# The six left-over channels of a depthwise convolution: four images in one matmul group instead of one image per group

## The chip, the cores and the metric

The kernel runs on one core of a Trainium2 chip. The metric is device time in microseconds (us) of one whole execution, all four layers of the network included. The time before is 3689.4 us, the median of three runs of 3689.62, 3683.67 and 3689.40 us.

## What is computed

The reference is four layers, each adding a function of a group-normalised input to its own input. The change lies in the first part of the first layer, which is cut here to what it computes:

```
x: 8 images, 384 channels, 32 x 32 pixels, float32
g = group_norm(x)                        # 32 groups of 12 channels, per image
for p in q, k, v:
    y = depthwise 3x3 convolution of g with dw_p, zero padding 1
    y = batch_norm(y)                    # mean and variance over all 8 images
    p = pw_p @ gelu(y)                   # 384 x 384 projection
attention over the 1024 pixels, 8 heads; projection; batch_norm; + x
then three further layers (experts, quantised convolution, attention with sampled keys)
```

The batch norm needs the mean and variance of each convolved channel over all eight images. So nothing behind the convolution can begin before the convolution of the last image is done. This first stage, all convolutions and their statistics, takes the first 384 us of the profile, and the projections and the attention of the first layer follow it.

## The kernel before

**How the convolution is laid out.** Channel 3p+c lies on partition p of chunk c, so an image is 128 partitions x 3 chunks x 1024 pixels. TensorE does the convolution for q, k and v at once. A group is 42 channels (`GC`): a tile `st` of 126 partitions holds these 42 channels three times, shifted by one row up, not at all, and one row down (`stack`, L311). A weight matrix of 126 x 126 then sums over the three rows and gives 42 x 3 output rows for q, k and v. Three matmuls, one for each column shift (`TAPS`, L334), add up in a PSUM bank, and this is done for the two halves of the image (`h`): six matmuls in the program for each group. In float32 each of them is two passes in the profile, so a group shows as twelve.

**Regular groups and the left-over group.** Nine groups of 42 channels (`NGC`) cover partitions 0 to 125. Partitions 126 and 127 hold six channels (`GR`) which fit in none, and each image has a tenth, left-over group for these, which comes fourth in image 0 and first in the others. Its tile `sr` has 3 x 6 = 18 rows in partitions 0 to 17 and the same 18 rows again in partitions 32 to 49. The first copy serves the first half of the image and the second copy the other half. In the program the matmuls of the two halves alternate (L382), but a scheduler gives out the final order on each engine. The program that is built keeps the alternation for images 2, 4, 6 and 7, and puts the three matmuls of the first half ahead of the three of the second for images 0, 1, 3 and 5.

**What happens around a group.** Six DMAs of SyncE's queue (SP) fill the left-over tile, three fill a regular one (L318, L327). ScalarE (ACT) copies each half from PSUM to the tile `y` (L397), VectorE (DVE) takes the batch-norm statistics of the half into `cst` (L398), and three DMAs on ACT's queue store q, k and v to the DRAM tensors `raw` (L406). On the last image, the stores of groups 5, 6 and 7 go by GpSimd's queue (POOL). For images 0, 2, 4 and 6 (`ON_V`), VectorE computes groups 6, 7 and 8 itself (`convolve`, L275), in 27 taps per image and three closing steps, two of these 30 behind each group. So TensorE has 60 regular and 8 left-over groups.

**Normalisation.** `norm` (L248) makes the group norm of an image in three steps: VectorE takes statistics of the loaded image `xa` into `mv_a`; TensorE sums them over groups in a tiny matmul `gna` (L114), VectorE makes `dm_a`, TensorE sums again in `gnb` (L125); VectorE and GpSimd (L95) make the scale, and ScalarE writes the scaled image to `pad` (L144), from which `stack` reads. These steps of later images are put between the groups of earlier ones. The list `work` holds the order of groups; `begins` (L341) sets behind which group each image's `norm` starts, about 11 groups ahead of its first use. A group's stack is issued 9 groups ahead (`AHEAD`). `y` has 9 buffers, `st` 10, `pad` 2, and the matmul results have 4 PSUM banks.

**End of the stage.** Behind each group of the last image, `bn_moments` (L152) reduces the statistics of that group over all images. `bn_params` (L156) then makes the scales of all ten groups, and two matmuls (`pmove`, L434, L438) bring them into the layout of the next stage.

**DMA semaphores.** In the built program the DMAs of SP and ACT use eight semaphores in turn. A DMA waits until the earlier one with its semaphore has landed. GpSimd's DMAs have eight of their own.

Of the kernel before, what the change touches and what calls it, by code (L numbers as in the profile page):

```python
# [7 lines left out]
F32 = mybir.dt.float32  # L8
# [4 lines left out]
B, C, H, W = 8, 384, 32, 32  # L13
# [4 lines left out]
NT8 = N // P  # L18


GC, NGC, GR = 42, 9, 6

# [30 lines left out]
def tile_kernel(ctx: ExitStack, tc: tile.TileContext, i: dict, out: bass.AP):  # L53
    nc = tc.nc
# [97 lines left out]
    def bn_moments(st, j, tiles):  # L152

        nc.vector.bn_aggr(tiles[0][:, j, :], st[:, j, :, :].rearrange("p a b -> p (a b)"))
# [49 lines left out]
    raw = [dram.tile([B, P, KC, N], F32, name=f"raw{v}") for v in range(3)]  # L204
    ss0 = const.tile([P, 3, 2, KC], F32, name="ss0")
    xmv = const.tile([P, B, KC, 2], F32, name="xmv")
    bn0 = bn_tiles(3 * GC, NGC + 1, "qkv")
    ON_V = (0, 2, 4, 6)
# [8 lines left out]
    with ExitStack() as pa:  # L217
        wa = pa.enter_context(tc.tile_pool(name="a_w", bufs=1))
        sa = pa.enter_context(tc.tile_pool(name="a_s", bufs=10))
# [7 lines left out]
        pads = []  # L227
# [4 lines left out]
        cst = wa.tile([3 * GC, NGC + 1, 2 * B, 6], F32, name="cst")  # L232
# [9 lines left out]
        cw = wa.tile([3 * GC, NGC, 3, 3 * GC], F32, name="cw_sb")  # L242
        nc.sync.dma_start(out=cw[:, :3], in_=i["cw"][:, :3])
        cwv = load_a("cwv")
        cwr = load_a("cwr")
# [65 lines left out]
        def stack(b, g):  # L311

            padf = pads[b % 2].rearrange("p c h w -> p c (h w)")
            if g < NGC:
                st = sa.tile([3 * GC, H, W], F32, tag="st", name=f"st{b}_{g}")
                c, t = divmod(g, 3)
                for dy in range(3):
                    stacked[0] = nc.sync.dma_start(  # L318
                        out=st[dy : 3 * GC : 3].rearrange("p h w -> p (h w)"),
                        in_=padf[t : 3 * GC : 3, c, dy * W : (dy + H) * W],  # L320
                    )
            else:
                st = sa.tile([32 + 3 * GR, H, W], F32, tag="sr", name=f"st{b}_{g}", bufs=2)
                for h in range(2):
                    for dy in range(3):
                        r = 32 * h + dy * GR
                        nc.sync.dma_start(  # L327
                            out=st[r : r + GR].rearrange("p h w -> p (h w)"),
                            in_=padf[3 * GC :, :, dy * W : (dy + H) * W],
                        )  # L330
            return st


        TAPS = [(1, 0, W, 0), (0, 0, W - 1, 1), (2, 1, W, 0)]  # L334
        AHEAD = 9
        groups = [(NGC, *range(NGC - 3 if b in ON_V else NGC)) for b in range(B)]

        groups[0] = (*groups[0][1:4], NGC, *groups[0][4:])
        work = [(b, g) for b in range(B) for g in groups[b]]

        begins = {max(2, work.index((b, NGC)) - AHEAD - 2): b for b in range(1, B)}  # L341
        sts, taps, todo, later, normed = {}, [], {}, list(work), {0}
        stacked = [None]

# [19 lines left out]
        for n, (b, g) in enumerate(work):  # L364
            if n in begins:
                b2 = begins[n]
                for k, f in enumerate(norm(b2)):
                    todo[n + k] = f, (b2 if k == 2 else 0)
                if b2 + 1 < B and b2 + 1 not in xts:
                    load_x(b2 + 1)  # L370
            if n in todo:
                f, b2 = todo.pop(n)
                f()
                normed.add(b2)
            stacks(n + AHEAD + 1)
            st = sts.pop((b, g))
            nch = GC if g < NGC else GR
            y = ya.tile([3 * nch, N], F32, tag="y", name=f"y{b}_{g}")
            pk = [bank(f"pk{b}_{g}_{h}") for h in range(2)]
            steps = [(h, k) for h in range(2) for k in range(3)]  # L380
            if g == NGC:
                steps = [(h, k) for k in range(3) for h in range(2)]  # L382
            for h, k in steps:
                dx, c0, c1, o0 = TAPS[k]
                rows = slice(h * (H // 2), (h + 1) * (H // 2))
                if g < NGC:
                    lhs, rhs = cw[:, g, dx, :], st[:, rows, c0:c1]
                else:
                    r = slice(32 * h, 32 * h + 3 * GR)
                    lhs, rhs = cwr[r, dx, :], st[r, rows, c0:c1]  # L390
                nc.tensor.matmul(  # L391
                    pk[h].rearrange("p (h w) -> p h w", w=W)[: 3 * nch, :, o0 : o0 + c1 - c0],
                    lhsT=lhs, rhs=rhs, start=(k == 0), stop=(k == 2),
                )
                if k == 2:
                    hs = slice(h * HALF, (h + 1) * HALF)
                    nc.scalar.copy(y[:, hs], pk[h][: 3 * nch, :])  # L397
                    nc.vector.bn_stats(cst[: 3 * nch, g, 2 * b + h, :], y[:, hs])  # L398
            for v in range(3):
                if g < NGC:  # L400
                    to, of = raw[v][b, g % 3 : 3 * GC : 3, g // 3, :], y[v : 3 * GC : 3, :]
                else:
                    to, of = raw[v][b, 3 * GC :, :, :], y[v * GR : (v + 1) * GR, :]

                queue = nc.gpsimd if b == B - 1 and g in (5, 6, 7) else nc.scalar
                queue.dma_start(out=to, in_=of)  # L406
            for _ in range(2):
                if taps:
                    taps.pop(0)()
            if b == B - 1:  # L410
                if g == 5:
                    load_b(0)
                bn_moments(cst, g, bn0)
        assert not taps and not todo and not xts


# [85 lines left out]
    with ExitStack() as pb:  # L502
# [179 lines left out]
        for v in range(2):  # L682
# [6 lines left out]
        steps = [  # L689
            (b, pr, h, kc)  # L690
            for b in range(B) for pr in ORDER[b + 1 == B] for h in range(2)
            for kc in range(0, NT8, NS)
        ]
# [66 lines left out]
        for k in range(2):  # L760
            qs = slice(k * HALF // 2, (k + 1) * HALF // 2)
            for m in range(KC):
                for c in range(KC):
                    nc.tensor.matmul(
                        pos[m][:, qs], lhsT=wo0[:, c, m * P : (m + 1) * P],
                        rhs=atts[B - 1][:, c, HALF:][:, qs], start=(c == 0), stop=(c == KC - 1),
# [18 lines left out]
    _, sco, sho = sc_o  # L785
# [51 lines left out]
    with tc.If(redo > 0):  # L837
        with ExitStack() as pb:
            wb = pb.enter_context(tc.tile_pool(name="e_w", bufs=1))
            work = [fetched[divmod(k, 2)] for k in range(5)]  # L840
# [11 lines left out]
            with tc.For_i(0, B) as bi:  # L852
                act = []
                for v in range(3):
                    g = work[v]
                    nc.sync.dma_start(
                        out=g, in_=raw[v][bass.ds(bi, 1)].rearrange("o p c n -> p (o c) n")
# [17 lines left out]
                for v in range(2):  # L875
                    ts = qp.tile([P, NPAIR0, N], F32, tag=f"qk{v}", name=f"qk{v}_e")
                    for pr in range(KC):
                        for h in range(2):
                            pq = bank(f"pq{v}_e{pr}_{h}")
                            for c in range(KC):  # L880
                                nc.tensor.matmul(
                                    pq, lhsT=w_in[v][:, c, pr * P : (pr + 1) * P],
                                    rhs=act[v][:, c, h * HALF : (h + 1) * HALF],
# [9 lines left out]
                for pr in range(NPAIR0):  # L893
                    qt, kt = qks[0][:, pr, :], qks[1][:, pr, :]
                    for h in range(2):
                        pav = bank(f"pav_e{pr}_{h}")
                        for j, r in enumerate(HR):
                            hd = 2 * pr + j
                            pt = qp.tile([P, NT8, HALF], F32, tag="pt", name=f"pt_e{pr}_{h}_{j}")
                            for qc in range(4):  # L900
# [11 lines left out]
                                p = pp.tile([P, N], F32, tag="p", name=f"p{nm}")  # L912
# [14 lines left out]
                            for kc in range(NT8):  # L927
# [5 lines left out]
                                    rhs=pt[:, kc, :],  # L933
# [3 lines left out]
                        hs = slice(h * HALF, (h + 1) * HALF)  # L937
# [913 lines left out]
def _layouts(a):  # L1851
    import numpy as np

    f = np.float32
    L = {}
# [18 lines left out]
    rest, ch = dw[:, NGC * GC :], np.arange(GR)  # L1874
    w = np.zeros((3, GR, 3, 3, GR), f)
    w[:, ch, :, :, ch] = rest.transpose(1, 2, 3, 0)
    w = w.reshape(3 * GR, 3, 3 * GR)
    dwv = np.stack([a[f"L0_conv_dw_{n}"].reshape(P, KC, 9)[:, KC - 1] for n in "qkv"])
    L["cwv"] = dwv.transpose(1, 0, 2)
    L["cwr"] = np.concatenate([w, np.zeros((32 - 3 * GR, 3, 3 * GR), f), w])  # L1880
    gb = np.zeros((3 * GC, 2, NGC + 1), f)
    for k, t in enumerate("gb"):
        v = np.stack([a[f"L0_conv_{t}_{n}"][order] for n in "qkv"])
# [83 lines left out]
```

## Time and profile before

| | |
|---|---|
| runs of the kernel before | 3689.62, 3683.67, 3689.40 us; median 3689.4 |
| the profiled execution | 3684.65 us, span 3682.8 us |
| TensorE (PE) busy | 3569.8 us, 97% of the span |
| VectorE, ScalarE, GpSimd busy | 48%, 35%, 5% of the span |
| mean granted TensorE clock | 0.982 |
| the first stage, to its last convolution matmul | 383 us; VectorE's last statistics start at 384.4 us |
| regular group's matmul passes `pk<-st,cw_sb` | 720 |
| left-over group's matmul passes `pk<-st,cwr_sb` | 96 |

Times are microseconds from the start of the span, means and medians in ns where marked. PE is a matmul pass and PEld its weight load. Matmuls overlap and their ends are modelled, so how far apart the weight loads start tells more than how long a matmul lasts. In the timeline, each row is start, duration, engine, line, operation, output<-input, count, and in brackets how long the engine was idle ahead of it and what ended that. `<-issue` names no wait that the profile could see. SPq and ACTq are the DMA queues of SyncE and ScalarE.

### The profile page before, as it was taken

What the parts mean: (1) busy time and instruction counts of PE and PEld (TensorE: products, weight loads), DVE (VectorE), ACT (ScalarE), POOL (GpSimd) and SP (SyncE); (2) the same over time, 40 slices, a digit from 0 to 9 for tenths busy, and PEclk for the clock granted to TensorE, in tenths of its full rate; (3) what the DMA queues carried; (4) which work ended last, traced back from release to release, by engine and by line L of the source; (5) the groups of instructions that cost most, each with busy time, mean ns of one, the idle gap of its engine ahead of it and who ended that gap; (6) DMA issues with size and microseconds to landing.
All of it is one profiled execution on the core that took longest, in us unless ns stands there. A gap on an engine that the chain in (4) does not pass through costs nothing.

```text
span 3682.8 us, 39040 instructions
## 1 busy us (share of the span) xinstructions
PE 3569.8 (97%) x15605; PEld 1525.8 (41%) x15605; DVE 1765.5 (48%) x2835; ACT 1273.8 (35%) x1524; POOL 196.1 (5%) x162
## 2 busy tenths in 40 slices
PE   7999999999999999999899999999999999999887
PEld 3444333333333333334434444445344444444434
DVE  6776223232323232323437637475663657547563
ACT  2222354545454444544322222323323232322222
POOL 0000100000000000000000010100102010010112
PEclk9999999999999999999999999999999999999898
DMA  6676311111212120212350010010101001010000
GB/s 205 229 253 228 146 55 34 66 42 58 64 37 64 39 77 27 76 27 74 112 218 23 33 52 20 33 54 33 37 20 48 37 33 43 28 52 20 0 35 18
DMA packets 88179, 253.33 MB, mean 69 GB/s; under 512 B 19114, under 2 KB 19706, under 8 KB 87602
## 3 DMA queue, kind: packets, MB, share of 16 engines
q1 hardware_dynamic: 75000, 211.35, 17.3%
q10 hardware_dynamic: 12408, 37.78, 3.0%
q8 instruction: 127, 2.08, 0.2%
q0 software_dynamic: 576, 1.55, 0.1%
q14 instruction: 68, 0.56, 0.0%
HBM read 133.39 MB, written 75.59 MB: 57 GB/s over the span
## 4 chain that ended last, share of the span: by engine, by line
PE 40%; DVE 9%; ACT 1%; DMA 0%; issue 0%; POOL 0%; DVEq 0%; POOLq 0%; ACTq 0%; SPq 0%
PE y L1327 12%; PE ph L1306 8%; DVE y L1402 6%; PE pq L1447 3%; PE pf L1737 3%; PE pw L1410 3%; PE pav L1637 2%; PE s L1621 2%; DVE hd L1292 1%; PE pss L1650 1%; PE pk L1595 1%; PE pv L1604 1%; PE xsb L1581 1%; PE px L1470 1%; DVE off L1517 1%; PE plog L1056 0%
## 5 line engine op out<-in xcount | busy, mean ns | idle before, releaser
L661 ACT ACTIVATE p<-s 128x1024 f32<-128x1024 f32 x512 | 496.4, 1021 | 508.7 <-PE s L654 508.4
L1327 PE MATMUL y<-hd,w_sb 128*128 128x512 f32 x1080 | 490.5, 600 | 3.5 <-DVE hd L1292 3.5
L669 PE MATMUL pav<-p,vt 64*64 64x512 f32 x4096 | 489.1, 590 | 0.0
L1306 PE MATMUL ph<-h,w_sb 128*128 128x512 f32 x1104 | 485.2, 594 | 1.0 <-DMA w_sb<-in_w_dram 0.9
L654 PE MATMUL s<-qk,qk 48*64 48x512 f32 x3072 | 371.9, 597 | 3.3 <-ACT p L661 3.3
L391 PE MATMUL pk<-st,cw_sb 126*126 126x512 f32 x720 | 320.5, 607 | 11.2 <-DMA st<-pad 10.4
L1306 PEld LDWEIGHTS ph<-h,w_sb 128*128 128x128 f32 x1104 | 207.5, 190 | 260.2 <-issue 255.9
L1327 PEld LDWEIGHTS y<-hd,w_sb 128*128 128x128 f32 x1080 | 198.5, 191 | 245.1 <-issue 233.5
L669 PEld LDWEIGHTS pav<-p,vt 64*64 64x64 f32 x4096 | 165.4, 133 | 276.3 <-issue 268.1
L630 DVE COPY ta<-pav 128x512 f32<-128x512 f32 (+1 forms) x65 | 44.2, 682 | 411.1 <-PE pav L669 411.1
L1402 DVE SCALAR_TENSOR_TENSOR y<-h,tap,y 128x961 f32<-128x961 f32 (+1 forms) x192 | 233.5, 1239 | 0.6
L1316 ACT ACTIVATE hd<-ph,b_sb 128x512 f32<-128x512 f32 x180 | 122.8, 682 | 316.0 <-PE ph L1306 316.0
L391 PEld LDWEIGHTS pk<-st,cw_sb 126*126 126x126 f32 x720 | 139.6, 196 | 183.9 <-issue 180.3
L1517 DVE SCALAR_TENSOR_TENSOR off<-q,dw_sb,off 128x225 f32<-128x225 f32 (+3 forms) x432 | 211.9, 546 | 1.6
L654 PEld LDWEIGHTS s<-qk,qk 48*64 48x64 f32 x3072 | 112.7, 133 | 227.0 <-issue 184.1
L78 DVE COPY qk<-pq 128x512 f32<-128x512 f32 x48 | 33.2, 692 | 292.6 <-PE pq L571 292.6
L397 ACT COPY y<-pk 126x512 f32<-126x512 f32 (+1 forms) x136 | 76.1, 584 | 252.5 <-DMA raw<-y 104.0
L1628 ACT ACTIVATE p<-s 128x1024 f32<-128x1024 f32 x96 | 93.3, 1022 | 191.0 <-PE s L1621 190.9
L1292 DVE TENSOR_TENSOR hd<-hd,cb 128x512 f32<-128x512 f32 x180 | 122.2, 684 | 47.9 <-ACT hd L1316 47.7
L1410 PE MATMUL pw<-y,upw 128*128 128x512 f32 x288 | 129.4, 603 | 9.3 <-DVE y L1402 9.3
L1737 PE MATMUL pf<-att,wp_sb 128*128 128x512 f32 x288 | 130.3, 607 | 4.3 <-DVE att L1664 3.8
L571 PE MATMUL pq<-g,wq_sb 128*128 128x512 f32 x288 | 131.0, 605 | 2.3 <-DMA wq_sb<-in_wq_dram 2.3
(292 smaller groups left out, 3830.1 us busy)
## 6 DMA issues: line engine op xcount, KB each, us to landing
g<-raw SPq DMA_DIRECT2D x72, 512.0 KB
st<-pad SPq DMA_DIRECT2D x180, 168.0 KB
raw<-y ACTq DMA_DIRECT2D x171, 168.0 KB
xa<-in_x_dram SPq DMA_DIRECT2D x24, 512.0 KB
xh<-in_x_dram SPq DMA_DIRECT2D x48, 256.0 KB
f<-in_x_dram SPq DMA_DIRECT2D x24, 512.0 KB
f<-o SPq DMA_DIRECT2D x24, 512.0 KB
o<-ot SPq DMA_DIRECT2D x42, 256.0 KB
```

The costliest lines, as they stand in the source:

```text
L391: nc.tensor.matmul(pk[h].rearrange("p (h w) -> p h w", w=W)[: 3 * nch, :, o0 : o0 + c1 - c0], lhsT=lhs, rhs=rhs, start=(k == 0), stop=(k = ...
L571: nc.tensor.matmul(pq, lhsT=w_in[v][:, c, pr * P : (pr + 1) * P], rhs=acts[b][v][:, c, h * HALF : (h + 1) * HALF], start=(c == 0), stop=(c ...
L654: nc.tensor.matmul(s[64 * k : 64 * k + 64, j * HALF : (j + 1) * HALF], lhsT=kt[r, k0 : k0 + 64], rhs=qt[r, h * HALF : (h + 1) * HALF], sta ...
L661: nc.scalar.activation(p, s, AF.Exp, scale=scale)
L669: nc.tensor.matmul(pav[k][64 * j : 64 * j + 64, :], lhsT=vts[b % 2][r, kc, 2 * hd : 2 * hd + 2, :].rearrange("p a b -> p (a b)"), rhs=p[r, ...
L1292: nc.vector.tensor_tensor(hd, hd, state["cb"], ALU.mult)
L1306: nc.tensor.matmul(ph, lhsT=w1[:, e, c, dc * P : (dc + 1) * P], rhs=state["h1"][c], start=(c == 0), stop=(c == KC - 1),)
L1327: nc.tensor.matmul(y, lhsT=w2[:, e, dc, m * P : (m + 1) * P], rhs=state[h, k], start=(k == 0), stop=(k == NE * KC - 1),)
L1402: nc.vector.scalar_tensor_tensor(d, f, tap2[:, c, t : t + 1], d, ALU.mult, ALU.add)
L1410: nc.tensor.matmul(pw[h], lhsT=upw2[:, c, m * P : (m + 1) * P], rhs=y[c][:, hs], start=(c == 0), stop=(c == KC - 1),)
L1517: nc.vector.scalar_tensor_tensor(d, f, dw3[:, t : t + 1], d, ALU.mult, ALU.add)
L1737: nc.tensor.matmul(pf[:, hs], lhsT=wp3[:, pr, m * P : (m + 1) * P], rhs=att[:, pr, hs], start=(pr == 0), stop=(pr == NPAIR3 - 1),)
```

## The change

The left-over channels of four images (`BR`) go into one tile of 4 x 18 = 72 partitions and are convolved as one group, with a block-diagonal weight matrix of 72 x 72. This group comes first in images 3 and 7; the other images have none. `left_over` issues three DMAs per image instead of six, behind the stack of group 1 (for images 3 and 7, ahead of group 0). The statistics of the group go into a tile `stl` first. GpSimd's queue then issues, for each of the four images, three stores to `raw` and one DMA that brings 18 rows of statistics to their place in `cst`: 16 DMAs for each such group. The reduction of the left-over statistics moves behind group 5 of the last image. The list `work` has 62 groups instead of 68, and the places where `norm` begins are computed anew.

```diff
-GC, NGC, GR = 42, 9, 6
+GC, NGC, GR, BR = 42, 9, 6, 4
...
+                if g == 1 and (b + 1) % BR:
+                    left_over(b)
             else:
-                st = sa.tile([32 + 3 * GR, H, W], F32, tag="sr", name=f"st{b}_{g}", bufs=2)
-                for h in range(2):
-                    for dy in range(3):
-                        r = 32 * h + dy * GR
-                        nc.sync.dma_start(
-                            out=st[r : r + GR].rearrange("p h w -> p (h w)"),
-                            in_=padf[3 * GC :, :, dy * W : (dy + H) * W],
-                        )
+                left_over(b)
+                st = lefts.pop(b // BR)
             return st
+        lefts = {}
+        def left_over(b):
+            k, j = divmod(b, BR)
+            if j == 0:
+                lefts[k] = sa.tile([3 * GR * BR, H, W], F32, tag="sr", name=f"sr{k}", bufs=2)
+            padf = pads[b % 2].rearrange("p c h w -> p c (h w)")
+            for dy in range(3):
+                r = (3 * j + dy) * GR
+                nc.sync.dma_start(
+                    out=lefts[k][r : r + GR].rearrange("p h w -> p (h w)"),
+                    in_=padf[3 * GC :, :, dy * W : (dy + H) * W],
+                )
...
-        groups = [(NGC, *range(NGC - 3 if b in ON_V else NGC)) for b in range(B)]
-        groups[0] = (*groups[0][1:4], NGC, *groups[0][4:])
+        groups = [
+            (*range(NGC, NGC + (b % BR == BR - 1)), *range(NGC - 3 if b in ON_V else NGC))
+            for b in range(B)
+        ]
         work = [(b, g) for b in range(B) for g in groups[b]]
-        begins = {max(2, work.index((b, NGC)) - AHEAD - 2): b for b in range(1, B)}
+        begins, n = {}, -1
+        for b in range(1, B):
+            n = max(n + 3, work.index((b, groups[b][0])) - AHEAD - 2)
+            begins[n] = b
...
-            nch = GC if g < NGC else GR
+            nch = GC if g < NGC else GR * BR
...
             if g == NGC:
-                steps = [(h, k) for k in range(3) for h in range(2)]
+                stl = wa.tile([3 * GR * BR, 2, 6], F32, tag="stl", name=f"stl{b}")
             for h, k in steps:
...
-                    r = slice(32 * h, 32 * h + 3 * GR)
-                    lhs, rhs = cwr[r, dx, :], st[r, rows, c0:c1]
+                lhs = cw[:, g, dx, :] if g < NGC else cwr[:, dx, :]
+                rhs = st[:, rows, c0:c1]
...
-                    nc.vector.bn_stats(cst[: 3 * nch, g, 2 * b + h, :], y[:, hs])
+                    st1 = cst[:, g, 2 * b + h, :] if g < NGC else stl[:, h, :]
+                    nc.vector.bn_stats(st1, y[:, hs])
+            for k in range(3 * BR if g == NGC else 0):
+                (j, v), r = divmod(k, 3), k * GR
+                b1 = b + 1 - BR + j
+                nc.gpsimd.dma_start(out=raw[v][b1, 3 * GC :, :, :], in_=y[r : r + GR, :])
+                if v == 0:
+                    nc.gpsimd.dma_start(
+                        out=cst[: 3 * GR, NGC, 2 * b1 : 2 * b1 + 2, :],
+                        in_=stl[r : r + 3 * GR, :, :],
+                    )
...
-                bn_moments(cst, g, bn0)
+                for k in () if g == NGC else (g, NGC) if g == 5 else (g,):
+                    bn_moments(cst, k, bn0)
```

In the built program of the changed kernel all six matmuls of the new group stand in the order first half, second half. On GpSimd its 16 DMAs stand behind the normalisation step of image 4, and those of the second group behind that of image 7. The order of the instructions behind this stage differs on no engine except for the place of one set of three small statistics DMAs on SP.

More of the change, by code (lines that the diff above doesn't have):

```diff
@@ L385, in tile_kernel @@
                 rows = slice(h * (H // 2), (h + 1) * (H // 2))
-                if g < NGC:
-                    lhs, rhs = cw[:, g, dx, :], st[:, rows, c0:c1]
-                else:
-                    r = slice(32 * h, 32 * h + 3 * GR)
-                    lhs, rhs = cwr[r, dx, :], st[r, rows, c0:c1]
+                lhs = cw[:, g, dx, :] if g < NGC else cwr[:, dx, :]
+                rhs = st[:, rows, c0:c1]
                 nc.tensor.matmul(
@@ L397, in tile_kernel @@
                     nc.scalar.copy(y[:, hs], pk[h][: 3 * nch, :])
[L398 to L403, printed above, removed]
+                    st1 = cst[:, g, 2 * b + h, :] if g < NGC else stl[:, h, :]
[9 more added lines that the diff above has]
+                    )
+            for v in range(3 if g < NGC else 0):
+                to, of = raw[v][b, g % 3 : 3 * GC : 3, g // 3, :], y[v : 3 * GC : 3, :]
                 queue = nc.gpsimd if b == B - 1 and g in (5, 6, 7) else nc.scalar
@@ L1876, in _layouts @@
     w[:, ch, :, :, ch] = rest.transpose(1, 2, 3, 0)
-    w = w.reshape(3 * GR, 3, 3 * GR)
+    w, wr = w.reshape(3 * GR, 3, 3 * GR), np.zeros((BR, 3 * GR, 3, BR, 3 * GR), f)
+    for j in range(BR):
+        wr[j, :, :, j] = w
     dwv = np.stack([a[f"L0_conv_dw_{n}"].reshape(P, KC, 9)[:, KC - 1] for n in "qkv"])
     L["cwv"] = dwv.transpose(1, 0, 2)
-    L["cwr"] = np.concatenate([w, np.zeros((32 - 3 * GR, 3, 3 * GR), f), w])
+    L["cwr"] = wr.reshape(3 * GR * BR, 3, 3 * GR * BR)
     gb = np.zeros((3 * GC, 2, NGC + 1), f)
```

## The prediction

> **What bounds the kernel now.** First the page: TensorE is busy for 97% of the span, so any time must come from its own queue. Then the stretches of the first stage (columns: stretch and length, busy time of PE, PEld, DVE, ACT, POOL with instruction counts, clock, DMA share, GB/s):
>
> ```profile
> 18.00:104.00 86.00, 79.49 (x176) 32.54 (x176) 63.65 (x99) 22.97 (x34) 1.11 (x2) 0.92 0.69 225
> 104.00:285.00 181.00, 174.06 (x425) 74.94 (x426) 135.02 (x202) 51.32 (x80) 3.89 (x4) 0.95 0.71 236
> 285.00:384.00 99.00, 98.72 (x244) 42.47 (x244) 60.39 (x85) 25.75 (x43) 6.12 (x10) 0.98 0.74 256
> ```
>
> PE is nearly full in all three, but its clock falls below 1.00. Then the weight loads, since their spacing is the true pace of PE. First the left-over group of image 6, whose halves alternate, and then that of image 3, whose halves stand one behind the other:
>
> ```profile
> 302.35 0.12 PEld L391 LDWEIGHTS pk<-st,cwr_sb 18*18 18x18 f32 x4 [0.73 <-issue]
> 302.80 0.10 PEld L391 LDWEIGHTS pk<-st,cwr_sb 18*18 18x18 f32 x2 [0.33 <-issue]
> ...
> 304.98 0.29 PEld L391 LDWEIGHTS pk<-st,cw_sb 126*126 126x126 f32 x2 [0.82 <-ACT y L397]
> ```
>
> ```profile
> 156.58 0.11 PEld L391 LDWEIGHTS pk<-st,cwr_sb 18*18 18x18 f32 x2
> 157.02 0.09 PEld L391 LDWEIGHTS pk<-st,cwr_sb 18*18 18x18 f32 x1 [0.34 <-issue]
> ...
> 160.96 0.30 PEld L125 LDWEIGHTS gnb_a<-dm_a,g_sb 128*128 128x128 f32 x2 [0.82 <-DVE cst L398]
> 161.18 0.30 PEld L391 LDWEIGHTS pk<-st,cw_sb 126*126 126x126 f32 x2
> 161.72 0.19 PEld L391 LDWEIGHTS pk<-st,cw_sb 126*126 126x126 f32 x1 [0.24 <-issue]
> 162.15 0.32 PEld L391 LDWEIGHTS pk<-st,cw_sb 126*126 126x126 f32 x1 [0.24 <-issue]
> 162.96 0.34 PEld L391 LDWEIGHTS pk<-st,cw_sb 126*126 126x126 f32 x1 [0.49 <-issue]
> 163.79 0.34 PEld L391 LDWEIGHTS pk<-st,cw_sb 126*126 126x126 f32 x1 [0.49 <-issue]
> ```
>
> The alternating group takes 304.98-302.35 = 2.63 us, two passes going at once. The serial one takes 161.18-156.58 = 4.60, and then four regular passes stand 0.82 apart instead of 0.42: half the clock. This follows every serial left-over group and no alternating one. Last, two weight loads that wait for a normalisation, and VectorE's statistics behind the second wait:
>
> ```profile
> 104.36 0.50 PEld L114 LDWEIGHTS gna_a<-mv_a,g_sb 128*128 128x128 f32 x2 [3.20 <-issue]
> 284.78 0.50 PEld L114 LDWEIGHTS gna_a<-mv_a,g_sb 128*128 128x128 f32 x2 [6.63 <-issue]
> ```
>
> ```profile
> 273.37 1.29 DVE L103 BATCH_NORM_STATS2 st_a<-xa 128x6 f32<-128x512 f32 x2 [8.20 <-DMA xa<-in_x_dram]
> ```
>
> PE works in order: if VectorE's mean is late, all convolutions stand still behind `gna`. At 284.78 the image itself was late.
>
> [...] The trace has nine such DMAs, 0.53 us of queue each (4.8 us), landing in 6.5 us.
>
> **Part 1: left-over matmuls.** Removed, from the first left-over weight load to the next regular one: images 0, 1, 3, 5 (serial) 6.82, 5.60, 4.60, 4.29; images 2, 4, 6, 7 four times 2.63. Sum 31.8. It holds four `gnb` of 0.42 us that stay: 30.1. It also holds `gnb`'s waits of 1.6 us for VectorE in images 0 and 1; a regular group of 5.04 us takes the place between `gna` and `gnb` and hides these. The slow passes behind the serial ones go too: 2.1 us each behind images 0 and 1, 1.65 each behind 3 and 5 = 7.5. Added: two groups of twelve passes at the regular 0.42 us = 10.1[...]. The clock under 72 rows is not in the trace: if they count as idle, each group is followed by 1.7 us more (3.4 us at half), 3.4 in all; if as work, nothing. I take nothing, because attention's 48- and 64-row passes keep the full clock (1.00 from 400 to 500 us). Net 27.5, if nothing else becomes late.
>
> **Part 2: what is late next.** *Image 1's stack.* Without its left-over group, image 0 ends early: group 2 begins at 33.2 as now, then four groups of 5.04 and two tiny matmuls of 0.42, so image 1 begins at 54.2 instead of 69.5. Its norm: `gnb` at 44, 1.5 us to the scale, ScalarE's three 1.24 us passes to 49.5. SP's stack DMAs go out at 1.34 us each there (9 in 12.06), land some 2.3 us later, and the three new left-over DMAs stand between the stacks of groups 1 and 2. Groups 0 and 1 come in time, group 2 some 2 us late. Cost 2.
>
> *Image 3's `gna`.* In the new order it stands behind group 4 of image 1, and VectorE does behind that group's second half: its statistics (with ScalarE's copy, 1.3), three taps of 1.24, six input statistics of 0.6, and the aggregates (0.5). That is 9.1 us in which PE has nothing ahead of it; now the wait is 3.2. Cost 5.9. Its half-clock stretch is there in both.
>
> *Image 7's `gna`.* Now 6.6 us late. In the new order VectorE does the six statistics nearly in one piece (some 5 us from the arrival at 273.4, against 11.2 now), but `gna` comes one group, 5 us, earlier. SP saves about as much as PE does (24 of its DMAs), so the image is about as late: wait 5.2. Gain 1.4. For images 4, 5 and 6 the mean's last input is a group at least two groups ahead of `gna`: nothing.
>
> **Part 3: ScalarE, VectorE, SP.** ScalarE loses 12 copies of 0.57 and 24 stores of about 0.8 us, VectorE 12 statistics of 0.67, SP 24 DMAs of 0.67. All lie beside PE, whose waits for these (0.1 to 0.9 us each) are inside the intervals above. Nothing more is counted.
>
> **Part 4: GpSimd's queue, a new wait.** Each group issues 16 DMAs. Behind the first eight, each waits for the landing of one eight ahead. Estimate from the nine DMAs in the trace: two times eight at 0.53, and two landings of 6.5 = 21 us as the upper end[...]. Behind them on GpSimd stand image 5's scale (for group 3) and the stores of groups 5 to 7 (for image 7). Image 5's `gnb` comes 30 us later: hidden. For image 7, VectorE's aggregate of the left-over channels waits for `cst`; it stands in the middle of group 4, 4.5 x 5.04 = 22.7 us behind the left-over group. Were it later, the work behind it on VectorE (one tap, two and nine statistics, five aggregates: 11 us) still has PE's 22.7 us to fit in: 11 more to spare. Cost 0; beyond some 34 us it would lie on the path one for one. Below nothing it can't go: nobody waited for these stores before. The order behind the stage is the old one, so the 3299 us from 384 on are counted unchanged.
>
> **Sum.** 27.5 - 2 - 5.9 + 1.4 = 21. On the profiled execution 3684.65 - 21 = 3663.7. That execution lies 4.7 us below the median of the runs, 3689.4, which itself is close to two of three; the mean of all four is 3686.8, and I forecast 3686.8 - 21 = 3666 us.
>
> **Rivals.**
> *A: the waits don't come.* If SP, relieved of 24 DMAs, brings images and stacks early and the scheduler's order does no harm, both losses (7.9) and image 7's rest (5.2 and its 1.65 of half clock) go: 21 + 14.8 = 36 gained, 3651. For it: SP's DMA issue runs almost without a break from 13 to 357 us. Against it: the 9.1 us are VectorE's work, not a transfer.
> *B: normalisation bounds the stage, and the gain turns into waits.* If `gna` of images 4 to 6, too, waited 4 us with 1.7 us of half clock each (17), and the 72-row groups halved the clock (3.4), the gain is 21 - 20.4 = 0.6: 3686. For it: two of seven waits stand there now. Against it: in the new order these three means are ready early.
> *C: slower, by GpSimd's queue.* If its 16 DMAs go one by one, each landing (6.5 us) ahead of the next, the left-over statistics of image 7 come after 16 x 6.5 = 104 us, 70 beyond the cover of 34: 3666 + 70 = 3736. It decides from 34/16 = 2.1 us per DMA and makes the kernel slower from (34+21)/16 = 3.4. Against it: three such DMAs were issued within 1.76 us at 371.15.
> *D: the change doesn't do what it says*, and the scheduler splits or repeats the groups: excluded, the built program has 62 groups.
>
> **Chances.** Faster, slower and same are parted at 0.2% (7.4 us), about what a measurement of this kernel can tell from no change. Forecast (13 to 29 us gained) 0.60; A (29 to 40) 0.18; between forecast and B (7.4 to 13) 0.10; B 0.07; C or the like 0.05. Faster 0.88, same 0.07, slower 0.05. The range from 3648 (A, taken from the lowest run, 3683.7) to 3680 (7 us gained) leaves out C, B and the far end of A.
>
> **What would show it.** `pk<-sr,cwr_sb` must have 24 passes instead of 96, 0.42 us apart. The last convolution pass must end about 21 us earlier than 383.5, and the first projection as much before 392.5. The regular passes behind the new groups should stand 0.42 apart (0.83 if 72 rows count as idle). Image 3's `gna` must show about 9 us of idle time, near 91 us. GpSimd's 16 DMAs should end within 21 us of their start, and no aggregate may wait for them. The prediction is wrong if `gna` of images 4 to 6 waits, if a stack is late beyond image 1, or if the gain isn't in the first 400 us.

## The result and the profile after

The changed kernel takes 3666.7 us, the median of five runs (3666.0 to 3667.7). The kernel before took 3688.9 beside it (3683.7 to 3689.6). The ratio is 0.9945 (95% interval 0.9934 to 0.9956), 22.2 us less by medians. The profiled execution took 3666.7 us with a span of 3664.9, 17.9 less than that of before (3682.8); the profiled execution of before was itself shorter than four of those five runs.

First the stretches of the first stage again, from the changed kernel's trace, with the columns as above:

```profile
18.00:104.00 86.00, 64.02 (x146) 28.86 (x147) 58.35 (x95) 19.47 (x28) 1.94 (x2) 0.88 0.74 244
104.00:285.00 181.00, 178.41 (x434) 79.98 (x433) 134.35 (x203) 55.39 (x83) 14.75 (x21) 0.99 0.72 240
285.00:384.00 99.00, 91.70 (x214) 40.53 (x213) 62.81 (x88) 31.29 (x45) 22.02 (x30) 0.95 0.79 277
```

The first stretch is worse than before: PE is busy for 64.0 us of 86 instead of 79.5, with a lower clock. The second is better: 178.4 of 181 instead of 174.1, at a clock of 0.99 instead of 0.95. The third already holds the start of the next stage. So the kernel falls behind until 104 us and then gains more than was forecast for that part.

The weight loads of the first merged group, in the timeline:

```profile
154.94 0.20 PEld L404 LDWEIGHTS pk<-sr,cwr_sb 72*72 72x72 f32 x2 [0.34 <-DVE ga_a L117]
...
159.22 0.14 PEld L404 LDWEIGHTS pk<-sr,cwr_sb 72*72 72x72 f32 x1 [0.27 <-issue]
159.63 0.19 PEld L126 LDWEIGHTS gnb_a<-dm_a,g_sb 128*128 128x128 f32 x1 [0.27 <-issue]
...
160.16 0.30 PEld L404 LDWEIGHTS pk<-st,cw_sb 126*126 126x126 f32 x2
160.70 0.19 PEld L404 LDWEIGHTS pk<-st,cw_sb 126*126 126x126 f32 x1 [0.24 <-issue]
161.13 0.19 PEld L404 LDWEIGHTS pk<-st,cw_sb 126*126 126x126 f32 x1 [0.24 <-issue]
```

Twelve passes in 159.63 - 154.94 = 4.7 us, and behind them regular passes 0.42 to 0.43 apart: full clock (1.00 from 160.2 to 170 us). So 72 rows do not "count as idle", my name for what half clock follows, as it followed PE's wait of 6.63 us at 284.78 before (0.51 from 286.0 to 288.5). The group of images 4 to 7 stands from 315.39 to 320.43 in the same way. Next `gna` of images 3 and 7, whose lines of before stood at 104.36 (wait 3.20) and 284.78 (wait 6.63):

```profile
100.20 0.50 PEld L115 LDWEIGHTS gna_a<-mv_a,g_sb 128*128 128x128 f32 x2 [14.43 <-issue]
...
101.65 0.34 PEld L404 LDWEIGHTS pk<-st,cw_sb 126*126 126x126 f32 x1 [0.52 <-issue]
102.50 0.34 PEld L404 LDWEIGHTS pk<-st,cw_sb 126*126 126x126 f32 x1 [0.52 <-issue]
...
264.18 0.19 PEld L115 LDWEIGHTS gna_a<-mv_a,g_sb 128*128 128x128 f32 x1 [0.23 <-issue]
```

Image 3's wait has grown to 14.4 us, with half clock behind it as before (0.50 from 101 to 106 us); image 7's is gone. VectorE's rows of the changed kernel tell why. The first two belong to image 3, the third to image 7:

```profile
94.71 2.70 DVE L104 BATCH_NORM_STATS2 st_a<-xa 128x6 f32<-128x512 f32 x4 [3.27 <-DMA xa<-in_x_dram]
...
98.45 1.28 DVE L104 BATCH_NORM_STATS2 st_a<-xa 128x6 f32<-128x512 f32 x2
...
254.57 1.29 DVE L104 BATCH_NORM_STATS2 st_a<-xa 128x6 f32<-128x512 f32 x2 [0.95 <-DMA xa<-in_x_dram]
```

Image 3 itself comes too late for PE, which has waited since 85.8: VectorE stands idle for it until 94.7. Image 7 arrives at 254.6 instead of 273.4, 18.8 us earlier, and its mean is ready ahead of PE. And at the start something is late that the prediction didn't name. PE's third group, the waits of SP's own queue up to 110 us (total, times, longest), and SP's timeline:

```profile
38.23 0.50 PEld L404 LDWEIGHTS pk<-st,cw_sb 126*126 126x126 f32 x2 [8.93 <-issue]
```

```profile
SPq L84 <- DMA raw<-y: 10.4, 1, 10.4
```

```profile
33.05 0.34 SPq L84 DMA_DIRECT2D ident_sb<-in_ident_dram  x1
33.44 7.87 SPq L319 DMA_DIRECT2D st<-pad  x9
```

Image 0's group 2 begins at 38.2 instead of 33.2. Its stack stands on SP's queue behind the load of `ident`, which waits 10.4 us for a store on ScalarE's queue. In the built program, the DMAs of both queues take eight completion semaphores in turn; three more DMAs ahead of `ident` moved it to the turn of a store that hadn't landed, and it was issued at 33.05. With these three behind group 5 (e6, below) it is issued at 20.18.

GpSimd's first sixteen DMAs:

```profile
162.22 0.73 POOL L417 DMA_DIRECT2D raw<-y  x1
164.53 0.54 POOL L419 DMA_DIRECT2D cst<-stl  x1 [1.57 <-DVE stl L412]
...
172.31 0.50 POOL L417 DMA_DIRECT2D raw<-y  x1 [0.49 <-DMA raw<-y]
```

They end 10.6 us after their start, the second set after 11.7 (322.2 to 333.9), and no aggregate waits for them. The last convolution is over 17 us earlier than before: the matmul `pmove` behind it begins at 371.64 instead of 388.95, and the first projection at 374.9 instead of 392.5. All of the gain lies in the first 400 us.

One row that the prediction didn't weigh is the end of SP's queue. These are the last stack loads, before and after:

```profile
344.23 12.32 SPq L318 DMA_DIRECT2D st<-pad  x12
```

```profile
319.21 11.47 SPq L319 DMA_DIRECT2D st<-pad  x9
```

Up to there SP issued 302 DMAs before, until 356.6 us, and 275 after, until 330.7. It is hardly ever at rest, but it is not busy issuing all the time: of the 343 and 317 us from 13 us on, issuing takes 231 and 205 (0.8 us for each DMA) and waiting 108 and 109, of which 69 and 77 are for stores on ScalarE's queue. How far SP is ahead shows better whether it holds PE up. Stacks are issued nine groups ahead; worked out from 5.04 us for a group, that is an estimated 45 to 50 us. Yet before, the last stack goes out only 26 us ahead of the last convolution pass (356.6 against 382.7), and after it 35 us (330.7 against 365.4). So before, SP was short of its lead while PE was 97% busy, and the change takes work off both. That is what the experiments have to part.

### The profile page after: what moved, and what is told of

The parts are those of the page before. It is cut to its first block, busy times and chain, and to the rows that moved or that the text cites. A ratio compares the mean times of both kernels' runs of the same rounds, so it can differ in the third digit from the quotient of the medians.

```text
span 3664.9 us, 38838 instructions
## 1 busy us (share of the span) xinstructions
PE 3542.1 (97%) x15533; PEld 1520.4 (41%) x15533; DVE 1759.0 (48%) x2823; ACT 1268.3 (35%) x1512; POOL 214.0 (6%) x194
## 4 chain that ended last, share of the span: by engine, by line
PE 40%; DVE 9%; ACT 1%; DMA 0%; issue 0%; POOL 0%; DVEq 0%; POOLq 0%; ACTq 0%; SPq 0%
PE y L1349 12%; PE ph L1328 8%; DVE y L1424 6%; PE pq L1469 3%; PE pf L1759 3%; PE pw L1432 3%; PE pav L1659 2%; PE s L1643 2%; DVE hd L1314 1%; PE pss L1672 1%; PE pk L1617 1%; PE pv L1626 1%; PE xsb L1603 1%; PE px L1492 1%; DVE off L1539 1%; PE plog L1078 0%
## 5 line engine op out<-in xcount | busy, mean ns | idle before, releaser
L404 PE MATMUL pk<-st,cw_sb 126*126 126x512 f32 x720 | 312.7, 595 | 17.7 <-DMA st<-pad 15.4
L79 DVE COPY qk<-pq 128x512 f32<-128x512 f32 x48 | 33.2, 692 | 292.2 <-PE pq L593 292.2
L1695 POOL TENSOR_TENSOR p<-p,p 128x1024 f32<-128x1024 f32 x48 | 113.0, 2354 | 355.1 <-ACT p L1650 355.1
```

What stands on the lines that cost most here:

```text
L404: nc.tensor.matmul(pk[h].rearrange("p (h w) -> p h w", w=W)[: 3 * nch, :, o0 : o0 + c1 - c0], lhsT=lhs, rhs=rhs, start=(k == 0), stop=(k = ...
```

## The experiments

Each was timed beside runs of the kernel before; "gained" and "lost" against the changed kernel compare its median with 3666.7.

**Passes taken out of the kernel before (e1).** Theory P is that of the prediction: PE's passes and its half clock are the price. Rival B: the normalisation bounds the stage.

```diff
...
+                if g < NGC:
+                    nc.tensor.matmul(
...
+                    of = pk[h] if g < NGC else st[:, rows].rearrange("p h w -> p (h w)")
-                    nc.scalar.copy(y[:, hs], pk[h][: 3 * nch, :])
+                    nc.scalar.copy(y[:, hs], of[: 3 * nch, :])
```

> The kernel before, with the left-over groups' matmuls left out: ScalarE copies rows of the input stack in their place, so the left-over channels of the output are not convolved; loads, copies, statistics and stores stay. My theory: TensorE's own passes are the price. 30.1 us of passes and 7.5 us of half clock go, less what comes back as waits for means and stacks that no longer have this cover: 30 us gained, 3659 (24 to 37 us gained, 3652 to 3665). Rival B (normalisation bounds the stage): the passes turn into waits, under 10 us gained, above 3679.

Measured: 3683.9 (before: 3687.6), ratio 0.9990 (0.9981 to 0.9999). With all 96 passes gone, 3.7 us are gained, and the interval reaches from 0.4 to 7. P fails here. The timeline shows the passes replaced by waits:

```profile
43.46 0.30 PEld L125 LDWEIGHTS gnb_a<-dm_a,g_sb 128*128 128x128 f32 x2 [3.12 <-ACT y L399]
47.10 0.50 PEld L392 LDWEIGHTS pk<-st,cw_sb 126*126 126x126 f32 x2 [3.34 <-issue]
69.21 0.50 PEld L125 LDWEIGHTS gnb_a<-dm_a,g_sb 128*128 128x128 f32 x2 [3.98 <-issue]
161.08 0.50 PEld L125 LDWEIGHTS gnb_a<-dm_a,g_sb 128*128 128x128 f32 x2 [3.38 <-DVE dm_a L119]
```

The left-over group stood between `gna` and `gnb` and covered VectorE's chain between the two. And SP still issues its 302 DMAs, until 356.7 us: the same as before to 0.2 us. In this trace the last convolution pass comes 3.8 us earlier than before, but even that is lost: the first projection begins at 393.0 (before: 392.5), since it waits 6.7 us for its weights, which SP loads behind the stacks. Two reasons for the small gain are possible: the order, and SP.

**Passes taken out of the changed kernel (e2)**, by the same edit.

> The changed kernel, with the matmuls of its two 72-row groups left out in the same way (left-over channels not convolved; loads, copies, statistics, stores and GpSimd's DMAs stay). My theory: two groups of 5.04 us go and nothing else, since no half clock follows them: 10 us gained on the changed kernel, 3656.7 (8 to 11). If the waits of the stage swallowed them (rival B): under 3 us gained, above 3663.

Measured: 3660.6 (3657.2 to 3664.5), ratio 0.9933 (0.9916 to 0.9949): about 6 us gained, 9.4 by the spans of the profiled executions. The median misses the 8 to 11 expected; small waits came back (2.4 us at one `gnb`, 3.5 us at another group). In the new kernel more than half of the removed PE time shows in the whole; in the old, a tenth (3.7 of an estimated 37.6 us).

**The order alone (e9).**

```diff
-        groups[0] = (*groups[0][1:4], NGC, *groups[0][4:])
+        groups = [(*g[1:6], NGC, *g[6:]) for g in groups]
...
-        begins = {max(2, work.index((b, NGC)) - AHEAD - 2): b for b in range(1, B)}
+        begins = {max(2, work.index((b, 0)) - AHEAD - 2): b for b in range(1, B)}
```

> The kernel before with only its order changed: each image's 18-row left-over group stands behind five groups of its image instead of ahead of them, so that regular groups stand between gna and gnb; loads, queues and the two tiles of 18 rows stay. Leaving the left-over passes out of the kernel before won only 3.7 us, since gnb then waited for VectorE with nothing to cover it. If the order is what the change needs to make its gain: the serial left-over groups become alternating ones of 2.63 us (31.8 - 21.0 = 10.8 us) and the half clock behind them goes (7.5): 10 to 20 us gained on before, 3668 to 3678. Rival (the merging of four images is the gain, the order nothing): within 4 us of before, 3685 to 3692.

Measured: 3693.2, ratio 1.0013 (1.0006 to 1.0020): slower. The edit did only part of what was expected: five of its eight left-over groups take 2.63 us, the other three 3.3 to 5.8, which makes 25.8 us instead of 31.8, and half clock follows two groups instead of four. Even this doesn't show in the time: it came back at `gna` of images 3, 5 and 7, with waits of 7.8, 5.7 and 8.2 us (before: 3.2, none and 6.6). The order alone gains nothing. In this trace SP's last stack comes 11 us later than before (367.6), with as many DMAs and 22 us more of waiting; why the order does this, and so why 5 us are lost, is not settled.

**The start (e6, e7, e8).** The changed kernel's two losses at the start are taken away, one at a time and then together.

```diff
-                if g == 1 and (b + 1) % BR:
+                if g == (5 if b == 0 else 1) and (b + 1) % BR:
```

> The changed kernel with image 0's three left-over DMAs issued behind the stack of group 5 instead of that of group 1. My theory: in the changed kernel these three DMAs shift the turn of the shared completion semaphores, so that the load of ident behind them waits 10.4 us for a store on ScalarE's queue, and the stack of image 0's group 2 stands behind it; without the shift group 2 begins near 33 instead of 38.2 us and its half-clock passes go. Image 3's mean waits for its image's transfer anyway, which takes back part: 0 to 7 us gained on the changed kernel, 3660 to 3667, with the wait of image 3's gna longer by what is gained ahead of it unless its image comes earlier too. Rival (the group is late because SP's queue is full): group 2 begins at 36 us or later, 3665 to 3668.

```diff
         load_x(2)
+        load_x(3)
         gb0 = load_a("gb0")
```

> The changed kernel with image 3's load issued right behind image 2's at the start instead of with the norm of image 2. My theory: the 14.4 us wait of image 3's gna in the changed kernel is that of the image's transfer and of the statistics behind it, not of VectorE's order: the wait falls below 5 us and its half clock (3.3 us) goes, 10 to 17 us gained, 3650 to 3657, less up to 6 us if the transfer delays the first stacks. Rival (VectorE's taps ahead of the mean): the wait stays above 9 us, less than 6 us gained.

> The changed kernel with both: left-over DMAs of image 0 late, image 3 loaded early. My theory: both start-up losses go and add up, 15 to 24 us gained on the changed kernel, 3643 to 3652. Rival (they are one and the same loss, of SP's queue): no more than the better of the two alone.

Measured: 3667.7, 3668.7 and 3667.9, ratios 0.9938 (0.9921 to 0.9955), 0.9947 (0.9931 to 0.9964) and 0.9939 (0.9923 to 0.9956). None gained, where 10 to 17 us were expected of e7 and 15 to 24 of e8, yet each edit did what it was meant to: in e6 group 2 begins at 32.5, in e7 image 3's `gna` doesn't wait, in e8 PE is busy for 75.1 us of the first 86 instead of 64.0. Weight loads of e8, `gna` of images 5 and 7, which waited for nothing in the changed kernel:

```profile
181.58 0.50 PEld L115 LDWEIGHTS gna_a<-mv_a,g_sb 128*128 128x128 f32 x2 [8.27 <-issue]
...
265.67 0.30 PEld L115 LDWEIGHTS gna_a<-mv_a,g_sb 128*128 128x128 f32 x2 [4.75 <-issue]
```

Some 13 us of waits for images come back. PE ran ahead, and its supply did not: in e8 the last stack goes out 29 us ahead of the last pass, in the changed kernel 35. This made theory S: SP's queue sets the pace of the images.

**SP's queue alone (e11, e12, e13).** In e11, nothing of the left-over channels is touched: 36 other small DMAs move from SP to GpSimd in the kernel before. e13 does the same in the changed kernel. e12 splits the changed kernel's left-over loads, with the same bytes.

```diff
-                    nc.sync.dma_start(
+                    nc.gpsimd.dma_start(
                         out=cst[v : 3 * GC : 3, 3 * (KC - 1) + t, 2 * b : 2 * b + 2, :],
```

> The kernel before with nothing of the left-over channels changed: the 36 little DMAs that bring VectorE's convolution statistics from vst to cst are issued by GpSimd instead of SP. Theory S (new: SP's queue sets the pace of the stage, 1.1 us for each of its 306 DMAs until the last stack, 95% busy; the change gains by taking 24 DMAs off it): 36 fewer, as much as the change or more: 15 to 30 us gained on before, 3658 to 3673. Theory P (of the prediction: TensorE's passes and half clock are what counts, SP's relief nothing): within 4 us of before, 3684 to 3692.

```diff
-                nc.sync.dma_start(
-                    out=lefts[k][r : r + GR].rearrange("p h w -> p (h w)"),
-                    in_=padf[3 * GC :, :, dy * W : (dy + H) * W],
-                )
+                for c in range(2):
+                    nc.sync.dma_start(
+                        out=lefts[k][r + 3 * c : r + 3 * c + 3].rearrange("p h w -> p (h w)"),
+                        in_=padf[3 * GC + c : 3 * GC + c + 1, :, dy * W : (dy + H) * W],
+                    )
```

> The changed kernel with each of its 24 left-over loads split into two of half the rows: the same bytes, 48 DMAs on SP's queue as before. Theory S: 24 x 1.1 = 26 us of SP's queue come back, 10 to 26 us slower than the changed kernel, 3677 to 3693. Theory P: no difference, 3664 to 3669.

> The changed kernel with the 36 DMAs from vst to cst issued by GpSimd instead of SP. Theory S: SP is freed of 36 more DMAs, 33 us of its queue; until something else bounds the stage, 8 to 30 us gained on the changed kernel, 3637 to 3659. Theory P: no difference, 3664 to 3669.

Measured: e12 3694.3, ratio 1.0022 (1.0014 to 1.0030), a little beyond the 3677 to 3693 of S. Twenty-four loads more on SP, with not a byte or a pass more, lose 27.6 us: all of the change's gain. Its last stacks and its three waits for images 3, 5 and 7:

```profile
361.04 9.18 SPq L319 DMA_DIRECT2D st<-pad  x9
```

```profile
104.67 0.50 PEld L115 LDWEIGHTS gna_a<-mv_a,g_sb 128*128 128x128 f32 x2 [17.32 <-issue]
...
196.65 0.50 PEld L115 LDWEIGHTS gna_a<-mv_a,g_sb 128*128 128x128 f32 x2 [8.64 <-issue]
...
285.49 0.50 PEld L115 LDWEIGHTS gna_a<-mv_a,g_sb 128*128 128x128 f32 x2 [10.41 <-issue]
```

The last stack comes 39 us later than in the changed kernel. Only 13 us of that are issuing (219 against 205 from 13 us on); 25 are waiting. The largest row of SP's waits (total, times, longest), first of the changed kernel, then of e12:

```profile
SPq L319 <- DMA raw<-y: 31.0, 30, 9.3
```

```profile
SPq L319 <- DMA raw<-y: 56.0, 30, 10.5
```

The waits for stores of ScalarE's queue, all rows together, grow from 77 to 103 us. So the edit does two things: it adds DMAs, and it shifts the turn of the semaphores. That the count is not all shows beside before: e12 has as many DMAs on SP up to its last stack (299 against 302) and 72 passes less on PE, in another order, and is still slower.

e11: 3674.5 (3669.6 to 3683.0), ratio 0.9967 (0.9953 to 0.9981): 12 us gained on before with every left-over pass in place. That is below the 15 expected, but outside what P allows. Where these 12 us lie its trace can't show: the profiled execution, span 3681.2, is the longest of its five and only 1.6 us shorter than that of before. e13: 3663.9, ratio 0.9937 (0.9921 to 0.9954), not to be told from the changed kernel: S's 8 us are missed. Its stretches say why. The second is that from 104 us:

```profile
18.00:104.00 86.00, 65.18 (x145) 29.12 (x146) 55.94 (x93) 19.49 (x28) 5.31 (x8) 0.87 0.74 243
104.00:285.00 181.00, 180.50 (x441) 81.19 (x441) 136.48 (x205) 55.66 (x84) 25.57 (x42) 0.99 0.75 252
```

SP's last stack is now issued at 313.5, 17 us earlier and 50 us ahead of the last pass, which is about all the lead that the program allows. But PE is busy for 180.5 us of 181 and can't use it, and the losses at the start, which this edit doesn't touch, stay (65 us of 86). So S alone fails as P alone did: what one of the two is relieved of becomes a wait for the other.

**Both relieved (e14).** The edits of e8 and e13 together: if two queues are the cause, the gain at the start, lost in e8, must now stay.

> The changed kernel with three edits together: image 0's left-over loads late, image 3 loaded early, and the 36 DMAs from vst to cst issued by GpSimd. Theory S+P (two queues, SP's and TensorE's, are both nearly full, and a loss taken from one comes back as a wait for the other): alone, the first two won nothing and the third 2.8 us; together the time won at the start is no longer taken back by late images, and TensorE stays full from 110 us on: 8 to 16 us gained on the changed kernel, 3651 to 3659. Rival (a third bound, such as VectorE's chain or the DMA engines' 75 to 83%): no more than the third edit alone, 3662 to 3666.

Measured: 3652.6 (3651.6 to 3655.3), ratio 0.9908 (0.9891 to 0.9924). It gains 14 us on the changed kernel, with edits that alone gave 0 and 3. SP's three DMAs that load image 7, first in e8 and then in e14:

```profile
252.88 3.18 SPq L170 DMA_DIRECT2D xa<-in_x_dram  x3
```

```profile
233.93 2.09 SPq L170 DMA_DIRECT2D xa<-in_x_dram  x3
```

The image is asked for 19 us earlier. No `gna` behind image 2 waits, the last stack has 44 us of lead, and the same stretches read:

```profile
18.00:104.00 86.00, 75.08 (x172) 33.68 (x173) 59.85 (x99) 23.18 (x33) 5.93 (x9) 0.94 0.73 247
104.00:285.00 181.00, 179.43 (x438) 80.35 (x437) 141.13 (x210) 54.65 (x85) 24.61 (x41) 1.00 0.78 260
```

Here the count accounts for most of the lead: of the 30 us by which the last stack is earlier than in e8, 24 are issuing. This version beats both kernels.

**GpSimd's queue (e3).**

```diff
-                nc.gpsimd.dma_start(out=raw[v][b1, 3 * GC :, :, :], in_=y[r : r + GR, :])
+                nc.scalar.dma_start(out=raw[v][b1, 3 * GC :, :, :], in_=y[r : r + GR, :])
...
-                    nc.gpsimd.dma_start(
+                    nc.scalar.dma_start(
                         out=cst[: 3 * GR, NGC, 2 * b1 : 2 * b1 + 2, :],
```

> The changed kernel with the 16 DMAs of each left-over group on ScalarE's queue instead of GpSimd's. My theory: the queue is no bound in either place; 16 issues of 0.8 us take 13 us of ScalarE twice[...]: 0 to 6 us slower than the changed kernel, 3667 to 3673. Rival C (GpSimd's queue costs the changed kernel something): faster than the changed kernel, below 3664.

Measured: 3693.8, ratio 1.0015 (1.0007 to 1.0023), 27 us lost. Rival C falls, but so does my 0 to 6. The 13 us of issuing were about right (14.6); that PE would hardly wait for them no trace had shown, and it was wrong: the program's pool for these results holds four tiles, which is two groups or 10 us. Rows of ScalarE and of PE's weight loads in e3:

```profile
163.57 0.28 ACTq L417 DMA_DIRECT2D raw<-y  x1
165.27 0.80 ACTq L419 DMA_DIRECT2D cst<-stl  x1
...
178.22 2.37 ACT L145 ACTIVATE pad<-xa,ss_a 128x1024 f32<-128x1024 f32 x2 [13.47 <-DMA raw<-y]
```

```profile
181.11 0.50 PEld L404 LDWEIGHTS pk<-st,cw_sb 126*126 126x126 f32 x2 [10.39 <-ACT y L410]
```

The sixteen issues take ScalarE from 163.6 to 178.2. Behind them stand two of the three scale passes of the next image and the copies that free PE's banks, so PE waits 10.4 us here and 11.3 behind the second group (at 358.9), with half clock after each (0.80 to 0.85 us between passes). On GpSimd little stands behind them: in the changed kernel its next instruction behind the first sixteen starts at 192.7, 20 us after their end. Of the two queues tried, the change needs this one.

**Two images in a group (e4).**

```diff
-GC, NGC, GR, BR = 42, 9, 6, 4
+GC, NGC, GR, BR = 42, 9, 6, 2
```

> The changed kernel with the left-over channels of two images in one group: four groups of 36 rows instead of two of 72. My theory: two more groups of 5.04 us, 3677 (3674 to 3680), if 36 rows count as work for TensorE's clock. If they count as idle like 18 rows: 1.7 us more behind each of four groups, 3684 (3681 to 3687). If the price of a group isn't what bounds the stage (rival B): within 3 us of the changed kernel.

Measured: 3681.6, ratio 0.9985 (0.9979 to 0.9992), 15 us lost against the changed kernel, within the range for "36 rows count as idle". Weight loads behind the second of its groups:

```profile
162.23 0.11 PEld L404 LDWEIGHTS pk<-sr,cwr_sb 36*36 36x36 f32 x1 [0.31 <-issue]
163.15 0.30 PEld L126 LDWEIGHTS gnb_a<-dm_a,g_sb 128*128 128x128 f32 x2 [0.81 <-DVE stl L412]
...
164.01 0.33 PEld L404 LDWEIGHTS pk<-st,cw_sb 126*126 126x126 f32 x1 [0.34 <-issue]
164.86 0.33 PEld L404 LDWEIGHTS pk<-st,cw_sb 126*126 126x126 f32 x1 [0.52 <-issue]
165.69 0.33 PEld L404 LDWEIGHTS pk<-st,cw_sb 126*126 126x126 f32 x1 [0.50 <-issue]
```

The passes inside the group stand 0.42 apart, those behind it 0.83: the half clock follows each of the four groups. With as many SP loads as the changed kernel, most of this loss lies on PE's side: two more groups (10.1 us) and four times 1.7 us of half clock are an estimated 17. The waits changed as well (`gna` of image 3 waits 3.4 us instead of 14.4, that of image 5 4.8 instead of none), so the agreement is not exact.

## Why the prediction was right, and where it wasn't

The time, 3666, was right within a microsecond, and so was the side. The account behind it was right only in part, and the closeness owes something to luck: the traces lie 17.9 us apart where 21 were forecast, the medians 22.2, and the forecast started from 3686.8, 2 us below the median of before.

*Part 1, passes.* The terms are as read: two groups of some 5 us (4.7 and 5.0), full clock behind 72 rows (1.00 from 160.2 to 170 and from 320.5 to 330), none of the half clock of the serial groups. That 72-row passes keep the pace of 126-row ones was an estimate; they stand 0.41 to 0.44 us apart. But the 27.5 us were called a net gain "if nothing else becomes late", and something does. The passes alone are worth 3.7 us in the kernel before (e1).

*Part 2.* Image 1's stack: no group of image 1 waits for it, so the 2 us were not lost. In its place image 0's group 2 came 5 us later with 2 us of half clock, by the turn of a semaphore that I had not looked at. Image 3's `gna`: cost 5.9 predicted, the wait grew by 11.2, for the image's transfer was late as well as VectorE. Image 7's `gna`: gain 1.4 predicted, 6.6 and its half clock of 1.65 measured. A wait of the first pass behind `gna` of image 6 costs 2.4, where nothing was counted. By `gna` of image 3 the kernel was about 1 us behind the old one, with one group of 5 us less done (104.36 - 100.20 - 5.04), where I had 8 us ahead. Behind it 18 us are gained where 13 were left of the 21. The loss of 9 at the start and the greater gain behind it cancel in good part: that is luck, not reckoning.

*Part 3 is the step that failed.* It says of ScalarE, VectorE and SP: "All lie beside PE" and "Nothing more is counted". With it falls the first sentence, that "any time must come from its own queue", meaning TensorE's. SP's 24 loads did not lie beside PE. With 24 more on the queue, 27.6 us are lost (e12); with 36 others taken off the kernel before, 12 are gained (e11). Part 2 did count the 24 loads once, for image 7: "SP saves about as much as PE does". But PE was ready for that `gna` only 9 us earlier than in the old kernel (264.2 against 284.8 - 6.6 = 278.2, less one group of 5.0 that no longer stands ahead of it), and the image came 18.8 us earlier: that is where the unforeseen gain lies. Rival A had read "SP's DMA issue runs almost without a break from 13 to 357 us", and I drew only the conclusion that waits might not come. The reading was too coarse as well: a third of that time SP isn't issuing but waiting, two thirds of this for the landing of ScalarE's stores. What shows that SP held PE up is its small lead and what e11, e12 and e14 do to the time.

*Part 4, GpSimd.* Right: some 11 us for each set, half the upper end of 21, and hidden. The upper end took 6.5 us for a landing, the median of the nine stores of 168 KB on GpSimd's queue before; those of 24 KB landed in 4.2 us and the 0.8 KB of statistics in 3.6 (medians). e3 shows that this price of nothing belongs to the queue and not to the work.

*Rivals.* B, that the gain turns into waits, is what e1 and e9 did, and also e12, where SP's loads are as many as before. A's waits at image 7 went, those at image 3 did not. C did not come.

Open: of the 1.1 to 1.3 us that SP takes for each DMA, some 0.8 are issuing (0.81 before, 0.79 after, 0.78 in e12), and the rest is waiting, which depends on whose semaphore comes up. No run here changes the turn alone with SP's relief kept, so how much of the 27.6 us of e12 is count and how much is turn is not shown; nor is it for e11. The stores that SP waits for come out of PE's own groups, so the two also hold each other up.

## What to carry to other kernels

When an engine is nearly full, look at the queue that feeds it as closely: count its instructions, part its issuing from its waiting, and see how far ahead of need its last one goes out. Where two hold each other up, relieving one alone can show little (3.7, 12, 3 or 0 us here, against some 33 from before to e14), so a null result of one edit doesn't clear it; relieve both, or add load to one and see whether the time moves. And before a DMA is added to a shared queue, look at what is queued behind it, at the start most of all.

## What was not expected of the hardware

- TensorE's clock: groups of 18 rows that took 4.3 to 6.8 us (before, e11) and all four groups of 36 rows (5.4 us and more, e4) are followed by half clock (0.83 us between passes instead of 0.42); groups of 18 rows that took 2.6 us and groups of 72 rows (5.0 to 5.2 us) are not. Where the border lies is open: of two groups of 18 rows in e9 that took 3.3 and 3.5 us, only the first is. Half clock follows waits as well, but not by their length alone: before, it follows 3.20 us of waiting at 104.36 (clock 0.50 from 104.7 to 110.5) and not 3.52 us at 33.19 (1.00 from 33 to 38).
- A DMA on SP's queue waited 10.4 us for a store on ScalarE's, with no data in common, only by the turn of the completion semaphores in this program.
- Splitting 24 DMAs into 48 of half the size moved SP's last stack from 330.7 to 370.2 us (275 DMAs up to there, then 299). The bytes were the same; of the 39 us, 13 are the issuing of more DMAs and 25 longer waits, most of them for ScalarE's stores.
- Sixteen DMAs take some 11 us of GpSimd's queue (0.5 us each while issuing) and 14.6 us of ScalarE's (e3).
